# Expert tiles of a mixture of experts recorded by readiness of the engines, with lists of free PSUM halves, in place of a lockstep rotation

## The chip, the cores and the metric

The kernel runs on one core of a Trainium2 chip. The metric is the device time of one execution in microseconds; several executions are made and their median is given.

## The reference, cut to what matters

Two transformer layers work on x of 16 sequences, 512 tokens and 128 channels, all in fp32. The last part of the second layer is a mixture of eight experts, of which each token takes the one with the largest gate value:

```python
idx = jnp.argmax(logits, axis=-1)
for e in range(E):                      # E = 8, D = 128, DF = 512
    m = (idx == e)[:, None].astype(xf.dtype)
    h = jax.nn.relu(xf @ W1[e] + b1[e])
    out = out + m * (h @ W2[e] + b2[e])
...
z = _layer_norm(y + _moe(y, ...), g2, be2)
...
x = x + gb * z
```

y is a layer norm too (with weights g1 and be1), and gb and the residual x differ from sequence to sequence. The change touches only how these last lines are carried out.

## The kernel before, in words

The program has three parts. The first (to about 780 us) does the first layer and the attention of the second for 16 sequences, four of them in flight. The second (to about 1065 us) does the attention inside the expert block and routes: for each token it finds the expert and writes the token's number into a list in DRAM (`order`), in the region of that expert. It leaves in DRAM a table `token_rows` with three rows of 128 values for each token: the normalized y (R_X), the gate row (R_G) and the residual row (R_RES).

The third part works the experts off. Each expert's list is cut into tiles of TS = 256 tokens. The number of tokens of an expert is known only on the device, so 8192 / 256 + 7 = 39 tiles are planned (NSLOT), and a few small operations (L1157 to L1222) find for each tile its expert and its tokens. `take` and `put` then hold the token numbers of each tile, as offsets for gathering and scattering.

`expert_tile(s)` (L1226) is a generator: a chain of 15 steps with a `yield` between them. For tile s:

- two indirect DMAs issued on GpSimd (POOL) gather the rows of 2 x 128 tokens into `x_in` (L1229);
- ScalarE (ACT) reads the number of the expert into a register (L1236) and copies that expert's weights, 1029 columns, from `ex` into `w` (L1238);
- TensorE (PE) turns the two halves of y into `x_ps`, a half of the PSUM tile `turn_ps` (L1242); ACT scales and shifts them into `y` (L1245);
- PE makes the hidden layer, four products of 128 x 256, into `h_ps` (L1249); VectorE (DVE) takes the maximum with minus the bias into `hid` (L1259), which is the ReLU without the bias;
- PE makes the output product, four accumulating products, into `o_ps`, a half of `out_ps` (L1263); DVE adds the bias and y into `acc` (L1272);
- PE turns `acc` back into `a_ps`, another half of `turn_ps` (L1276); `stats` (L1012) makes the layer norm's figures on DVE (L1017, L1019, L1024, L1280) and ACT (the square root, L1022);
- ACT normalizes into `z` (L1284), DVE multiplies by the gate row and adds the residual (L1292, L1293);
- two indirect DMAs issued on POOL scatter the rows into the output (L1296).

The halves of `turn_ps` and `out_ps` go by the parity of s (`s % 2`). `h_ps` is a tile of a pool with two buffers. `x_in` has six buffers, `w`, `y` and `z` four, the others three.

What sets the order is `staggered(chains, 3)` (L151): in lockstep it advances every running chain by one step, and every third step it starts a new one. The tile framework takes the instructions in the order in which they are recorded, finds the waits between them from the tiles that they read and write, and places them on the engines; it can move an instruction ahead of others on its engine.

The first two parts are recorded by another helper, `queued(chains, apart, width)` (L118). It keeps up to `width` chains, each with a due time, and advances the one that is due first. A chain yields what its step costs: "V1.2" is 1.2 us of DVE (V), P is PE, A is ACT, G is GpSimd, D a delay on no engine; parts with | run beside each other, parts with ; after each other, and a part with + isn't waited for. The helper books these costs on each engine and so sets the chain's next due time. `taken(free)` (L217) is a step that a chain repeats, at a cost of "D0.5", until a list has a free entry, which it then takes.

Of the kernel before, what the change touches and what calls it, by code (L numbers as in the profile page):

```python
# [21 lines left out]
F32 = mybir.dt.float32  # L22
# [6 lines left out]
P = 128  # L29
B, T, C = 16, 512, 128  # L30
# [3 lines left out]
NFC = DF // P  # L34
# [14 lines left out]
DEN_EPS = 1e-6  # L49
NEG = -1e30  # L50
TS = 2 * P
NSLOT = B * T // TS + NE - 1
REGION = B * T
R_X, R_G, R_RES, R_END = np.cumsum([0, C, C, C]).tolist()
E_W1, E_W2, E_NB1, E_OUT, E_END = np.cumsum([0, DF, DF, NFC, 1]).tolist()
# [62 lines left out]
def queued(chains, apart, width):  # L118

    chains, running, begin, free = iter(chains), [], 0.0, 0.0
    until = dict.fromkeys("PVAG", 0.0)
    while True:
        while len(running) < width and (chain := next(chains, None)) is not None:
            running.append([max(begin, free), chain])
            begin = running[-1][0] + apart
        if not running:  # L130
            return
        first = min(running, key=lambda entry: entry[0])
        took = next(first[1], None)
        if took is None:
            assert first is running[0], "a chain's buffers are those of the one that ends first"
            running.remove(first)
            free = first[0]
            continue
        for stage in took.split(";"):
            ends = [first[0]]  # L140
            for part in stage.split("|"):
                engine, us = part.lstrip("+")[0], float(part.lstrip("+")[1:])
                end = max(first[0], until.get(engine, 0.0)) + us
                if engine in until:
                    until[engine] = end
                if part[0] != "+":
                    ends.append(end)
            first[0] = max(ends) + 0.1


def staggered(chains, apart):  # L151

    chains, running, step = iter(chains), [], 0
    while True:
        if step % apart == 0 and (chain := next(chains, None)) is not None:
            running.append(chain)
        if not running:
            return
        for chain in list(running):
            if next(chain, chain) is chain:  # L160
                running.remove(chain)
        step += 1


@with_exitstack
def tile_adaln(ctx: ExitStack, tc: tile.TileContext, x, wa, wb, vec, wex, const, out):
# [50 lines left out]
    def taken(free):  # L217
        while not free:
            yield "D0.5"
        return free.pop(0)  # L220
# [790 lines left out]

    def stats(pool, src, n, tag):  # L1012

        st = pool.tile([P, n, 6], F32, tag=tag + "_st", name="st", bufs=3)
        mv = pool.tile([P, n, 2], F32, tag=tag + "_mv", name="mv", bufs=3)
        for g in range(n):
            nc.vector.bn_stats(st[:, g, :], src[:, g * C : (g + 1) * C])  # L1017
        for g in range(n):
            nc.vector.bn_aggr(mv[:, g, :], st[:, g, :])  # L1019
        yield  # L1020
        rs = pool.tile([P, n], F32, tag=tag + "_rs", name="rs", bufs=3)
        nc.scalar.activation(rs, mv[:, :, 1], AF.Sqrt, bias=lneps)  # L1022
        yield
        nc.vector.reciprocal(rs, rs)  # L1024
        return mv, rs

# [196 lines left out]

    out_rows = out.rearrange("b t c -> (b t) c")

    def expert_tile(s):  # L1226
        x_in = tp.tile([P, 2, R_END], F32, tag="x_in", name="x_in", bufs=6)
        for a in range(2):
            nc.gpsimd.indirect_dma_start(  # L1229
                out=x_in[:, a],  # L1230
                out_offset=None,
                in_=token_rows,
                in_offset=bass.IndirectOffsetOnAxis(ap=take[:, a, s : s + 1], axis=0),
            )
        yield
        e = nc.scalar.value_load(expert_i[0:1, s : s + 1], min_val=0, max_val=NE - 1)  # L1236
        w = tp.tile([P, E_END], F32, tag="w", name="w", bufs=4)
        nc.scalar.copy(w, ex[:, bass.ds(e, 1), :].rearrange("p a k -> p (a k)"))  # L1238
        yield
        x_ps = turn_ps[:, 0, s % 2]  # L1240
        for a in range(2):
            nc.tensor.transpose(x_ps[:, a * P : (a + 1) * P], x_in[:, a, R_X:R_G], ident)  # L1242
        yield
        y = tp.tile([P, TS], F32, tag="y", name="y", bufs=4)
        nc.scalar.activation(y, x_ps, AF.Identity, bias=v(V_BE1), scale=v(V_G1))  # L1245
        yield
        h_ps = sp.tile([P, NFC, TS], F32, tag="h_ps", name="h_ps")
        for f in range(NFC):
            mm(  # L1249
                h_ps[:, f, :],  # L1250
                lhsT=w[:, E_W1 + f * P : E_W1 + (f + 1) * P],
                rhs=y,
                start=True,
                stop=True,
            )
        yield

        hid = tp.tile([P, NFC, TS], F32, tag="hid", name="hid", bufs=3)
        tt(hid, h_ps, w[:, E_NB1:E_OUT].unsqueeze(2).to_broadcast([P, NFC, TS]), ALU.max)  # L1259
        yield  # L1260
        o_ps = out_ps[:, s % 2]
        for f in range(NFC):
            mm(  # L1263
                o_ps,
                lhsT=w[:, E_W2 + f * C : E_W2 + (f + 1) * C],
                rhs=hid[:, f, :],
                start=f == 0,
                stop=f == NFC - 1,
            )
        yield  # L1270
        acc = tp.tile([P, TS], F32, tag="acc", name="acc", bufs=3)
        stt(acc, o_ps, w[:, E_OUT:E_END], y, ALU.add, ALU.add)  # L1272
        yield
        a_ps = turn_ps[:, 1, s % 2]
        for a in range(2):
            nc.tensor.transpose(a_ps[:, a * P : (a + 1) * P], acc[:, a * P : (a + 1) * P], ident)  # L1276
        yield
        mv, rs = yield from stats(tp, a_ps, 2, "last")
        off = tp.tile([P, 2], F32, tag="off", name="off", bufs=3)
        stt(off, mv[:, :, 0], -1.0, rs, ALU.mult, ALU.mult)  # L1280
        yield
        z = tp.tile([P, 2, C], F32, tag="z", name="z", bufs=4)
        for a in range(2):
            nc.scalar.activation(  # L1284
                z[:, a],
                a_ps[:, a * P : (a + 1) * P],
                AF.Identity,
                bias=off[:, a : a + 1],
                scale=rs[:, a : a + 1],
            )  # L1290
        yield
        tt(z, z, x_in[:, :, R_G:R_RES], ALU.mult)  # L1292
        tt(z, z, x_in[:, :, R_RES:R_END], ALU.add)  # L1293
        yield
        for a in range(2):
            sent = nc.gpsimd.indirect_dma_start(  # L1296
                out=out_rows,
                out_offset=bass.IndirectOffsetOnAxis(ap=put[:, a, s : s + 1], axis=0),
                in_=z[:, a],
                in_offset=None,  # L1300
                bounds_check=B * T - 1,
                oob_is_err=False,
            )
            apart("out", sent.ins)

    staggered((expert_tile(s) for s in range(NSLOT)), 3)


# [90 lines left out]
```

## Time and profile before

| What | us |
|---|---|
| median of three runs | 1390.64 (1388.35 to 1391.99) |
| the profiled execution, its own time | 1304.73 |
| its span, first to last instruction | 1302.9 |
| first gather of an expert tile | 1080.64 |
| first scatter | 1105.76 |
| last gather | 1277.83 |
| last scatter | 1299.09 |

The profiled execution is 85.9 us shorter than the median of the runs. In the stretch of 178 us from 1106 to 1284, in which the tiles follow each other evenly, PE is busy 147.4 us, POOL 136.9, DVE 118.3 and ACT 92.3, at a granted TensorE clock of 1.00.

How to read the profile: a row of the timeline or of the groups names the engine, the line of the kernel, the operation, the tile written and the tiles read, the number of instructions, and in brackets the idle time of the engine just before and what ended it ("<-DVE hid L1259"). "issue" is time in which the engine waited for nothing that the profile shows. The 0.30 us between two indirect DMAs on POOL are of that kind. PEld is the loading of weights into TensorE, which lies beside PE's products. A product in fp32 appears as two records, so that four products make eight.

### The profile page before, as it was taken

The numbers are of one execution on the slowest core, as the hardware profiler recorded it, in microseconds if no ns is written. First come the engines' busy times: TensorE is split into PE (matmuls) and PEld (weight loads), VectorE is DVE, ScalarE is ACT, GpSimd is POOL, SyncE is SP. The second block draws the span as 40 slices with busy tenths as digits, with TensorE's granted clock in tenths as the row PEclk, the third lists the DMA queues.
The fourth block names the chain that finished last, engine by engine and source line by source line (L and its number), as shares of the span: only waits on it lengthen the run. The fifth ranks groups of instructions, "written<-read, shape, count | busy, mean of one in ns | idle before, by whom it ended". The sixth has DMA issues, their size and how long they took to land.

```text
span 1302.9 us, 37480 instructions
## 1 busy us (share of the span) xinstructions
PE 1022.4 (78%) x15605; PEld 742.7 (57%) x15605; DVE 814.8 (63%) x2335; ACT 645.7 (50%) x1116; POOL 576.5 (44%) x632
## 2 busy tenths in 40 slices
PE   3789899787798798898898786867687815888885
PEld 2467666565566566565765564655465514666663
DVE  7455877656666758667557765256667723666664
ACT  0535566455463555464365443255666613555552
POOL 5222434425323426324324343225555644777775
PEclk9877898888998889898689978587878757999998
DMA  4412323322332422333223224204423112333331
GB/s 156 114 33 52 86 52 88 73 60 58 86 57 64 95 49 71 81 65 85 58 56 74 48 52 159 66 26 36 41 40 49 24 19 77 97 98 97 101 98 39
DMA packets 155275, 90.62 MB, mean 70 GB/s; under 512 B 77070, under 2 KB 142609, under 8 KB 154976
## 3 DMA queue, kind: packets, MB, share of 16 engines
q1 hardware_dynamic: 144960, 65.36, 23.2%
q0 software_dynamic: 9568, 19.62, 5.5%
q8 instruction: 123, 2.02, 0.7%
q10 hardware_dynamic: 576, 3.23, 0.6%
q14 instruction: 48, 0.39, 0.1%
HBM read 47.96 MB, written 31.68 MB: 61 GB/s over the span
## 4 chain that ended last, share of the span: by engine, by line
PE 40%; DVE 27%; POOL 12%; ACT 7%; DMA 6%; issue 6%; SPq 0%; POOLq 0%; ACTq 0%; DVEq 0%
PE bank L464 5%; PE out_ps L1263 5%; PE h_ps L1249 4%; PE bank L533 4%; DVE q L406 3%; PE bank L630 3%; DVE hid L1259 3%; DVE sc L555 3%; POOL rs L403 2%; POOL order L1131 2%; PE scores L551 2%; DVE st L397 2%; DVE inc L595 2%; PE bank L617 2%; PE bank L420 2%
## 5 line engine op out<-in xcount | busy, mean ns | idle before, releaser
L533 PE MATMUL bank<-kh,q 32*32 32x128 f32 x4096 | 107.5, 315 | 14.4 <-DVE h L520 5.9
L406 DVE TENSOR_SCALAR q<-x,mv,rs 128x128 f32<-128x128 f32 x256 | 86.8, 396 | 42.2 <-POOL rs L403 42.1
L501 ACT ACTIVATE kh<-k,con 128x512 f32<-128x512 f32 x128 | 84.4, 715 | 50.3 <-POOL k L755 43.1
L533 PEld LDWEIGHTS bank<-kh,q 32*32 32x32 f32 x4096 | 81.9, 119 | 35.7 <-issue 9.5
L1263 PE MATMUL out_ps<-hid,w 128*128 128x256 f32 x312 | 77.6, 391 | 28.6 <-DVE hid L1259 28.3
L555 DVE TENSOR_TENSOR sc<-scores,con 128x1024 f32<-128x1024 f32 x64 | 77.4, 1210 | 35.5 <-PE scores L551 35.2
L607 POOL COPY states<-inc 32x576 f32<-32x576 f32 x64 | 43.7, 682 | 121.3 <-DVE inc L595 119.2
L1296 POOL DMA_INDIRECT out_x<-z,put x78 | 79.2, 1015 | 39.5 <-ACT rs L1022 17.9
L551 PE MATMUL scores<-ident,sc 128*128 128x128 f32 x512 | 80.7, 304 | 17.3 <-DVE sc L555 14.9
L542 ACT COPY sc<-bank 128x512 f32<-128x512 f32 x128 | 68.6, 588 | 46.9 <-PE bank L533 46.6
L1229 POOL DMA_INDIRECT x_in<-token_rows,take x78 | 77.3, 991 | 26.3 <-issue 18.9
L1131 POOL DMA_INDIRECT order<-con,idx x64 | 62.9, 983 | 50.6 <-DVE idx L1128 18.6
L551 PEld LDWEIGHTS scores<-ident,sc 128*128 128x128 f32 x512 | 66.0, 158 | 31.2 <-DVE sc L555 16.9
L1259 DVE TENSOR_TENSOR hid<-h_ps,w 128x1024 f32<-128x1024 f32 x39 | 47.8, 1225 | 54.4 <-PE h_ps L1249 54.4
L1263 PEld LDWEIGHTS out_ps<-hid,w 128*128 128x128 f32 x312 | 56.2, 190 | 43.1 <-DVE hid L1259 37.1
L630 PE MATMUL bank<-states,q 128*32 128x144 f32 x960 | 75.6, 425 | 6.0 <-POOL states L607 5.4
L422 ACT ACTIVATE h<-bank,mod 128x512 f32<-128x512 f32 x48 | 37.2, 775 | 83.1 <-PE bank L420 82.8
L1249 PE MATMUL h_ps<-y,w 128*128 128x256 f32 x312 | 76.2, 388 | 1.3 <-ACT y L1245 1.2
L1238 ACT COPY w<-ex 128x1029 f32 x39 | 40.8, 1052 | 67.2 <-DVE acc L1272 36.6
L617 PE MATMUL bank<-v_heads,sc 128*32 128x36 f32 x4096 | 62.3, 207 | 14.5 <-DVE sc L555 7.6
L607 ACT COPY states<-inc 32x576 f32<-32x576 f32 x64 | 42.8, 669 | 61.7 <-DVE inc L595 61.1
L617 PEld LDWEIGHTS bank<-v_heads,sc 128*32 128x32 f32 x4096 | 50.8, 115 | 37.8 <-issue 17.9
(248 smaller groups left out, 2539.6 us busy)
## 6 DMA issues: line engine op xcount, KB each, us to landing
v_rows<-values SPq DMA_DIRECT2D x32, 288.0 KB
v_chunks<-values SPq DMA_DIRECT2D x128, 72.0 KB
v_heads<-v_rows SPq DMA_DIRECT2D x128, 72.0 KB
gated<-mod_rows SPq DMA_DIRECT2D x16, 448.0 KB
x<-in_x SPq DMA_DIRECT2D x16, 256.0 KB
token_rows<-gated SPq DMA_DIRECT2D x16, 256.0 KB
token_rows<-ex SPq DMA_DIRECT2D x16, 256.0 KB
h_rows<-q SPq DMA_DIRECT2D x16, 256.0 KB
```

Of the source, the lines that this page charges most:

```text
L406: ts(xn[:, g, :], X[b][:, g, :], mv[:, g, 0:1], rs[:, g : g + 1], ALU.subtract, ALU.mult,)
L501: nc.scalar.activation(t[:, :, n, :], k.rearrange("p (n s) -> p n s", s=CH), AF.Copy, scale=con[:, K_HEAD + n : K_HEAD + n + 1],)
L533: mm(groups(s_ps[r])[c * CH : (c + 1) * CH, n], lhsT=by_block[rows, at], rhs=kh[rows, at].rearrange("p m s -> p (m s)"), start=True, stop= ...
L551: nc.tensor.transpose(groups(st_ps[:, r])[:, n], groups(sc[:, 2 * rr + r])[:, n], ident)
L555: tt(sc[:, 2 * rr : 2 * rr + 2].rearrange("p r (n t) -> p (r n) t", t=CH), st_ps.rearrange("p r (n t) -> p (r n) t", t=CH), causal.unsquee ...
L607: copy(state[rows, r], inc[rows])
L617: mm(o_ps[a][c * CH : (c + 1) * CH, k0 : k0 + RH * HV], lhsT=groups(sc[:, r])[:, g, c * CH : (c + 1) * CH], rhs=vh[:, g * NC + c, :, r * H ...
L630: mm(o_ps[a][c * CH : (c + 1) * CH, n * NH * HV : (n + 1) * NH * HV], lhsT=q.rearrange("p (n s) -> p n s", s=CH)[:, at_chunk(ch)], rhs=sta ...
L1131: put = nc.gpsimd.indirect_dma_start(out=order, out_offset=bass.IndirectOffsetOnAxis(ap=idx[:, g : g + 1], axis=0), in_=con[:, K_TOK + 4 * ...
L1249: mm(h_ps[:, f, :], lhsT=w[:, E_W1 + f * P : E_W1 + (f + 1) * P], rhs=y, start=True, stop=True,)
L1259: tt(hid, h_ps, w[:, E_NB1:E_OUT].unsqueeze(2).to_broadcast([P, NFC, TS]), ALU.max)
L1263: mm(o_ps, lhsT=w[:, E_W2 + f * C : E_W2 + (f + 1) * C], rhs=hid[:, f, :], start=f == 0, stop=f == NFC - 1,)
```

## The change

`staggered` is deleted, and the expert tiles are recorded by `queued`, with six chains in flight and 4.0 us between the starts of two. Every step yields its cost. The halves of PSUM are no longer chosen by parity: four lists hold the two free halves each of the turned input, the hidden product, the output product and the turned output. A chain takes a half ahead of the product that writes it and gives it back behind the last instruction that reads it. `h_ps` becomes two tiles of one buffer each; `turn_ps` and `out_ps` stay one tile each. The buffers of `x_in` and `z` go to eight, those of `w`, `y`, `hid`, `acc`, `off` and of the tiles of `stats` to seven. In `stats` two yields get costs. The computation is the same.

```diff
+SLOTS = 6
...
-def staggered(chains, apart):
...
-        st = pool.tile([P, n, 6], F32, tag=tag + "_st", name="st", bufs=3)
-        mv = pool.tile([P, n, 2], F32, tag=tag + "_mv", name="mv", bufs=3)
+        st = pool.tile([P, n, 6], F32, tag=tag + "_st", name="st", bufs=SLOTS + 1)
+        mv = pool.tile([P, n, 2], F32, tag=tag + "_mv", name="mv", bufs=SLOTS + 1)
...
-        yield
+        yield "V1.0"
...
+    free_in, free_hid, free_out, free_back = [0, 1], [0, 1], [0, 1], [0, 1]
+    h_banks = [sp.tile([P, NFC, TS], F32, tag=f"h_ps{n}", name="h_ps", bufs=1) for n in range(2)]
+
     def expert_tile(s):
-        x_in = tp.tile([P, 2, R_END], F32, tag="x_in", name="x_in", bufs=6)
+        x_in = tp.tile([P, 2, R_END], F32, tag="x_in", name="x_in", bufs=SLOTS + 2)
...
-        yield
+        yield "G2.2;D3.0"
         e = nc.scalar.value_load(expert_i[0:1, s : s + 1], min_val=0, max_val=NE - 1)
-        w = tp.tile([P, E_END], F32, tag="w", name="w", bufs=4)
+        w = tp.tile([P, E_END], F32, tag="w", name="w", bufs=SLOTS + 1)
         nc.scalar.copy(w, ex[:, bass.ds(e, 1), :].rearrange("p a k -> p (a k)"))
-        yield
-        x_ps = turn_ps[:, 0, s % 2]
+        yield "A1.2"
+        at = yield from taken(free_in)
+        x_ps = turn_ps[:, 0, at]
...
-        yield
+        yield "P0.4"
-        y = tp.tile([P, TS], F32, tag="y", name="y", bufs=4)
+        y = tp.tile([P, TS], F32, tag="y", name="y", bufs=SLOTS + 1)
         nc.scalar.activation(y, x_ps, AF.Identity, bias=v(V_BE1), scale=v(V_G1))
-        yield
-        h_ps = sp.tile([P, NFC, TS], F32, tag="h_ps", name="h_ps")
+        free_in.append(at)
+        yield "A0.6"
+        at = yield from taken(free_hid)
+        h_ps = h_banks[at]
...
+        yield "P1.9"
...
         tt(hid, h_ps, w[:, E_NB1:E_OUT].unsqueeze(2).to_broadcast([P, NFC, TS]), ALU.max)
-        yield
-        o_ps = out_ps[:, s % 2]
+        free_hid.append(at)
+        yield "V1.3"
+        at = yield from taken(free_out)
+        o_ps = out_ps[:, at]
...
+        yield "P2.0"
...
         stt(acc, o_ps, w[:, E_OUT:E_END], y, ALU.add, ALU.add)
-        yield
-        a_ps = turn_ps[:, 1, s % 2]
+        free_out.append(at)
+        yield "V0.5"
+        at = yield from taken(free_back)
+        a_ps = turn_ps[:, 1, at]
...
-        yield
+        free_back.append(at)
+        yield "A0.9"
         tt(z, z, x_in[:, :, R_G:R_RES], ALU.mult)
         tt(z, z, x_in[:, :, R_RES:R_END], ALU.add)
-        yield
+        yield "V0.7"
...
+        yield "G2.2"
...
-    staggered((expert_tile(s) for s in range(NSLOT)), 3)
+    queued((expert_tile(s) for s in range(NSLOT)), 4.0, SLOTS)
```

More of the change, by code (lines that the diff above doesn't have):

```diff
@@ L148, in queued @@
             first[0] = max(ends) + 0.1
-def staggered(chains, apart):
[L153 to L162, printed above, removed]
 @with_exitstack
@@ L1019, in stats @@
             nc.vector.bn_aggr(mv[:, g, :], st[:, g, :])
-        yield
-        rs = pool.tile([P, n], F32, tag=tag + "_rs", name="rs", bufs=3)
+        yield "V1.0"
+        rs = pool.tile([P, n], F32, tag=tag + "_rs", name="rs", bufs=SLOTS + 1)
         nc.scalar.activation(rs, mv[:, :, 1], AF.Sqrt, bias=lneps)
-        yield
+        yield "A0.3"
         nc.vector.reciprocal(rs, rs)
@@ L1255, in expert_tile @@
             )
-        yield
-        hid = tp.tile([P, NFC, TS], F32, tag="hid", name="hid", bufs=3)
+        yield "P1.9"
+        hid = tp.tile([P, NFC, TS], F32, tag="hid", name="hid", bufs=SLOTS + 1)
         tt(hid, h_ps, w[:, E_NB1:E_OUT].unsqueeze(2).to_broadcast([P, NFC, TS]), ALU.max)
-        yield
-        o_ps = out_ps[:, s % 2]
+        free_hid.append(at)
+        yield "V1.3"
+        at = yield from taken(free_out)
+        o_ps = out_ps[:, at]
         for f in range(NFC):
@@ L1269, in expert_tile @@
             )
-        yield
-        acc = tp.tile([P, TS], F32, tag="acc", name="acc", bufs=3)
+        yield "P2.0"
+        acc = tp.tile([P, TS], F32, tag="acc", name="acc", bufs=SLOTS + 1)
         stt(acc, o_ps, w[:, E_OUT:E_END], y, ALU.add, ALU.add)
-        yield
-        a_ps = turn_ps[:, 1, s % 2]
+        free_out.append(at)
+        yield "V0.5"
+        at = yield from taken(free_back)
+        a_ps = turn_ps[:, 1, at]
         for a in range(2):
             nc.tensor.transpose(a_ps[:, a * P : (a + 1) * P], acc[:, a * P : (a + 1) * P], ident)
-        yield
+        yield "P0.4"
         mv, rs = yield from stats(tp, a_ps, 2, "last")
-        off = tp.tile([P, 2], F32, tag="off", name="off", bufs=3)
+        off = tp.tile([P, 2], F32, tag="off", name="off", bufs=SLOTS + 1)
         stt(off, mv[:, :, 0], -1.0, rs, ALU.mult, ALU.mult)
-        yield
-        z = tp.tile([P, 2, C], F32, tag="z", name="z", bufs=4)
+        yield "V0.4"
+        z = tp.tile([P, 2, C], F32, tag="z", name="z", bufs=SLOTS + 2)
         for a in range(2):
@@ L1290, in expert_tile @@
             )
-        yield
+        free_back.append(at)
+        yield "A0.9"
         tt(z, z, x_in[:, :, R_G:R_RES], ALU.mult)
         tt(z, z, x_in[:, :, R_RES:R_END], ALU.add)
-        yield
+        yield "V0.7"
         for a in range(2):
```

## The prediction

> **What bounds the kernel now.** I read the busy time by stretches first. The expert tiles run from the first gather at 1080.64 us to the end at 1302.9, about 222 us. In their steady part no engine is full: per 10 us PE is busy 8.24, POOL 7.78, DVE 6.79, ACT 5.36, and the TensorE clock is granted at 1.00 (columns: stretch, length, PE, PEld, DVE, ACT, POOL, clock, DMA share, GB/s).
>
> ```profile
> 1185.00:1195.00 10.00, 8.24 (x42) 6.84 (x41) 6.79 (x21) 5.36 (x11) 7.78 (x8) 1.00 0.34 96
> ...
> 1275.00:1285.00 10.00, 8.66 (x39) 6.36 (x38) 6.31 (x20) 3.33 (x8) 7.07 (x7) 1.00 0.37 93
> ```
>
> So I looked at two loops. The chain of waits in order of time shows a ring of PE and DVE (start, us, what).
>
> ```profile
> 1184.17 1.99 PE out_ps L1263 x8
> 1186.16 1.74 PE h_ps L1249 x8
> 1187.93 1.24 DVE hid L1259
> 1189.21 1.99 PE out_ps L1263 x8
> ```
>
> One turn, 1184.17 to 1189.21, takes 5.04 us: the lockstep order puts the hidden product of one tile behind the output product of the one before and makes both wait for the ReLU. The timeline of POOL shows the second loop.
>
> ```profile
> 1094.47 0.95 POOL L1229 DMA_INDIRECT x_in<-token_rows,take  x1 [0.30 <-issue]
> 1105.76 1.03 POOL L1296 DMA_INDIRECT out_x<-z,put  x1 [10.34 <-ACT rs L1022]
> 1107.09 1.00 POOL L1296 DMA_INDIRECT out_x<-z,put  x1 [0.31 <-issue]
> 1108.40 1.00 POOL L1229 DMA_INDIRECT x_in<-token_rows,take  x1 [0.30 <-issue]
> ...
> 1279.11 1.14 POOL L1296 DMA_INDIRECT out_x<-z,put  x1 [0.30 <-ACT y L1245]
> 1280.56 1.00 POOL L1296 DMA_INDIRECT out_x<-z,put  x1 [0.30 <-issue]
> ...
> 1285.33 0.98 POOL L1296 DMA_INDIRECT out_x<-z,put  x1 [1.20 <-ACT rs L1022]
> ...
> 1289.64 0.98 POOL L1296 DMA_INDIRECT out_x<-z,put  x1 [2.05 <-ACT rs L1022]
> ...
> 1299.09 0.98 POOL L1296 DMA_INDIRECT out_x<-z,put  x1 [1.81 <-issue]
> ```
>
> Each tile needs two gathers and two scatters, each about 1.0 us of POOL with 0.30 between. From tile 0's first scatter (1105.76) to tile 33's (1279.11) lie 33 tiles or 132 issues in 173.35 us: 1.313 us an issue, 5.25 a tile, and no gap there is above 0.31. POOL, at 5.25, is slower than the ring of 5.04. That it shows 78% is only because the 0.30 is not counted. It stands still only at the ends: 10.34 us after 12 gathers, and 1.20, 2.05 and 1.84 among the last scatters.
>
> [...] all 156 are on POOL, so they can't be shared out by a new order. [...] the trace shows the price, 1.31 us an issue. [...]
>
> **The change part by part.** Everything ahead of the first gather is the same program, instruction by instruction and wait by wait, so 1080.64 us stand. Nothing is removed or added within the tiles either: 156 indirect DMAs, the same products, the same copies. What changes is order and buffers.
>
> (1) Gathers ahead. With eight x_in buffers in place of six the built POOL order holds 16 gathers ahead of the first scatter, not 12, and 16 scatters at its end, not 12. Gathers alone are 1.257 us apart (1080.64 to 1094.47 in 11 steps), so 16 end near 1080.64 + 16 x 1.257 = 1100.8, inside the old stand of 10.34 us. Four issues so leave the saturated part: 4 x 1.313 = 5.25 us.
>
> (2) The first scatter. Tile 0's chain (gather, turn, hidden and output product, statistics, z) is as long as before. On DVE the built order has the two products by the gate (L1292, L1293 of before) directly behind the third ReLU, ahead of the next tile's two BN_STATS (0.50 us together). I take 0.5 us: scatter at 1105.3.
>
> (3) The rest is counted at POOL's pace: 140 issues are left, 139 steps from the first to the last: 1105.3 + 139 x 1.313 = 1287.8. The unexplained 1.81 ahead of the very last issue is 1.5 over the usual 0.30; I leave it in: 1289.3. Before it was 1299.09. Without any new stall this is 9.8 us less; about 4 of it are the stands of the tail, which go since 16 scatters (21 us) now lie behind the last gather, and cover most of the last tile's chain (about 4.1 us from issue to landing in the chain of waits, then 13.2 us, 1281.95 to 1295.14).
>
> (4) What the new order makes late. The rotation by parity becomes lists of free halves, but turn_ps and out_ps stay one tile each, and the waits in the built program are on the whole tile: a bias add (L1272) whose tile has its half complete still waits for the output product written into the other half, if that is ahead of it in the recorded order. In 10 places two bias adds now follow each other on DVE, the first waiting for the second's product. One such wait is one more output product, 1.99 us. Queued behind it on DVE are that tile's statistics, and on ACT its z; who waits is POOL with the scatter. The first comes at tiles 2 and 3, when POOL has no work in hand: I charge 2.0 in full. At tiles 8 and 9 the scatters stand as four in a row ahead of four gathers, so tile 8's may be late again: between 0 and 2, taken 1.0. From then on I charge nothing for the other pairs: the products alone start 1.83 + 1.73 + 0.18 + 0.18 = 3.9 us a tile (distances between starts of L1263, L1249, L1276, L1242), 1.3 below POOL, and with eight gathers ahead a tile has 42 us (8 x 5.25) for its chain. If that cover is gone each costs up to 2 us. Tail: the last chain just fits; 0 to 2.6, taken 1.2.
>
> (5) More w, y, hid, acc, st, z buffers: ACT's wait of the w copy for acc (36.6 us in the waits) goes, worth 0, since POOL, not ACT, bounds. ACT loses no time for the register loads that the built order draws forward: in before two of them and more lie inside waits.
>
> Sum: -9.8 + 2.0 + 1.0 + 1.2 = -5.6 us. Of the profiled execution (1304.73, span 1302.9 and 1.8 around it) this makes 1299.1. The median of the runs, 1390.64, is 85.9 above that execution, and no view says where. I carry the difference over unscaled: 1385.0. (Scaled by 1.066 it would be 5.9.)
>
> **The rivals.** B, much faster: the runs are 6.6% longer than the profiled execution; if that is a slower TensorE, the ring and not POOL bounds them. At 0.8 of the clock a turn is (1.99 + 1.74) / 0.8 + 1.31 = 5.97 us, 0.72 over POOL, and setting it free is worth up to 34 x 0.72 = 24 us more: 1361. For it: PE makes up 40% of the chain over the program, and the granted clock has a mean of 0.861. Against it: in this stage the clock is 1.00, a uniform slowdown moves POOL as well, and the pairs of (4) grow with the products.
>
> C, slower: late outputs. POOL is always behind, so time it loses to a late z never comes back. If all ten pairs hit it for 2.0 us, that is 20 against the 9.8: +10.2, 1401. It decides from 9.8 us of stands, and is slower beyond measurement from 14. For it: in before z was ready every 5.04 us, evenly, which no list of readiness keeps. Against it: the slack of 1.3 us a tile outside the first few tiles.
>
> D, nothing: stands of 6 to 14 us eat the gain; 1389 or so. The estimates of durations that drive the new order (2.2 us for two gathers) are below the 2.6 of the trace, so POOL is believed ahead of where it is.
>
> **How the numbers follow.** About 0.3%, 4.2 us, is what a measurement of this kernel can tell from no change. The forecast A, 1382 to 1388, has 0.58, of which a fifth lies under 4.2 us; B 0.12; D 0.18; C 0.12. Faster: 0.46 + 0.12, say 0.57; same 0.12 + 0.18, say 0.31; slower 0.12. The range reaches from the middle of B to the edge of C: 1367 to 1394.
>
> **What would show it.** Right: 16 gathers spaced 1.26, first scatter near 1105, then 1.31 a step with one stand of about 2 us near the third tile's scatter, last scatter near 1293 to 1294; the ring of L1263, L1249 and L1259 no longer unbroken in the chain, POOL in its place. Wrong: stands of POOL all along (C, D), or a steady pace below 5.25 a tile, which would mean that the 1.31 is not POOL's own. Wrong too if the first scatter comes later than 1106 because ACT copies w for eight tiles ahead of tile 0's z.

## The result, and the profile after

The changed kernel is slower, by less than 2%. On the runs beside which the prediction was made it takes 1410.4 us in the median (1408.2 to 1411.8) against 1389.5 of the kernel before: a ratio of 1.016, 95% interval 1.012 to 1.020. Measured twice more it took 1396.2 against 1383.3 (1.008, 1.005 to 1.011) and 1395.6 against 1380.6 (1.009, 1.006 to 1.012). The prediction had 1385.0. The ratios here and below are estimated from the executions outside a slower state and need not be the quotients of the medians.

One thing has to be known for all numbers below: the executions fell on three chips, on which the same program does not take the same time. On the first chip (e0 to e3 and all runs named f and g) the kernel before takes 1381 to 1392 us in the median, and on the third (h1 and h2) 1392.0. On the second (e4 to e7) it takes 1304.7 us (63 runs, 1290 to 1316). For the first timed runs and for the profile that the prediction read the chip is not on record: by their times the runs (1389.5 and 1410.4) are of the first chip's kind and the profile (1304.73) is of the second's.

The profiled execution of the changed kernel takes 1410.47 us, its span 1408.7. Its timeline of POOL (start, us busy, what, and in brackets the idle time just before) answers to the one shown of before:

```profile
1139.06 0.95 POOL L1220 DMA_INDIRECT x_in<-token_rows,take  x1 [0.30 <-issue]
1140.31 0.95 POOL L1220 DMA_INDIRECT x_in<-token_rows,take  x1 [0.30 <-issue]
1154.97 1.03 POOL L1295 DMA_INDIRECT out_x<-z,put  x1 [13.71 <-issue]
1156.31 1.01 POOL L1295 DMA_INDIRECT out_x<-z,put  x1 [0.31 <-issue]
1157.62 1.00 POOL L1220 DMA_INDIRECT x_in<-token_rows,take  x1 [0.30 <-issue]
...
1171.75 1.01 POOL L1295 DMA_INDIRECT out_x<-z,put  x1 [6.61 <-issue]
...
1370.40 1.01 POOL L1295 DMA_INDIRECT out_x<-z,put  x1 [6.85 <-ACT rs L1009]
...
1404.91 0.98 POOL L1295 DMA_INDIRECT out_x<-z,put  x1 [0.85 <-issue]
```

The 16 gathers ahead are there, 1.26 us apart as predicted. But the first scatter comes 33.5 us after the first gather (1121.46), not 24.7, and then POOL does not keep going: it stands for 13.7, 6.6, 6.9 us and more. One issue still costs 1.31 us where it follows another. In the groups of the page the idle time ahead of the scatters is 105.6 us:

```profile
L1295 POOL DMA_INDIRECT out_x<-z,put x78 | 78.3, 1004 | 105.6 <-issue 45.7
```

The busy times by stretches (columns as before: stretch, length, PE, PEld, DVE, ACT, POOL, clock, DMA share, GB/s) show two kinds of stretch instead of one:

```profile
1185.00:1195.00 10.00, 7.83 (x37) 6.03 (x36) 4.68 (x16) 4.17 (x9) 7.82 (x8) 1.00 0.34 94
1225.00:1235.00 10.00, 3.03 (x16) 2.10 (x14) 3.54 (x16) 3.74 (x7) 7.68 (x8) 0.91 0.43 118
1275.00:1285.00 10.00, 6.33 (x19) 5.05 (x20) 3.52 (x13) 4.21 (x8) 2.98 (x3) 0.53 0.18 57
```

In the second line PE, DVE and ACT are each busy for a third of the time while POOL issues its eight; in the third the TensorE clock is 0.53, and PE's 19 records fill 6.3 us. What happens there is seen in the timeline around 1230 us:

```profile
1228.14 1.89 PE L1243 MATMUL h_ps<-y,w 128*128 128x256 f32 x8
...
1229.87 0.38 PE L1234 MATMUL turn_ps<-ident,x_in 128*128 128x128 f32 x2
...
1230.30 1.00 POOL L1295 DMA_INDIRECT out_x<-z,put  x1 [0.30 <-ACT rs L1009]
1231.60 1.00 POOL L1220 DMA_INDIRECT x_in<-token_rows,take  x1 [0.30 <-DMA out_x<-z,put]
1232.90 0.98 POOL L1220 DMA_INDIRECT x_in<-token_rows,take  x1 [0.30 <-issue]
1234.19 1.01 POOL L1295 DMA_INDIRECT out_x<-z,put  x1 [0.30 <-issue]
1234.92 1.22 DVE L1253 TENSOR_TENSOR hid<-h_ps,w 128x1024 f32<-128x1024 f32 x1 [4.68 <-remote]
...
1237.05 0.56 ACT L1237 ACTIVATE y<-turn_ps,vec_sb 128x256 f32<-128x256 f32 x1 [7.01 <-remote]
...
1237.66 1.65 PE L1243 MATMUL h_ps<-y,w 128*128 128x256 f32 x3 [7.41 <-ACT y L1237]
```

The hidden product ends at 1230.03 by the trace, and DVE is free, but the ReLU that waits for it starts at 1234.92. The turn of x_in ends at 1230.25, and y, which waits for it, starts at 1237.05. In the trace "remote" means that the wait ended with a semaphore's update just before the start, but that no instruction's end fits that update. I call such a wait late: a DVE or ACT instruction among the expert tiles starts more than 0.5 us after both its own engine is free and the last product that the built program makes it wait for has ended. This execution has 24 of them, 66 us together, and in the first profile of before there is not one. PE stands through them, and its clock falls: the granted clock is 1.00 from 1137 to 1140 us and 0.50 from 1143 to 1149, and the eight records (four products) of L1259 that took 1.99 us at 1134.64 take 3.78 at 1145.26, after 5.66 us of idle PE. A caution: the ends of the products in this profile are modelled. So one such wait alone can't tell whether the product is late or only the news of it.

### The profile page after: what moved, and what is told of

The parts are those of the page before. It is cut to its first block, busy times and chain, and to the rows that moved or that the text cites. A ratio compares the mean times of both kernels' runs of the same rounds, so it can differ in the third digit from the quotient of the medians.

```text
span 1408.7 us, 37474 instructions
## 1 busy us (share of the span) xinstructions
PE 1052.5 (75%) x15605; PEld 755.5 (54%) x15605; DVE 812.4 (58%) x2335; ACT 639.2 (45%) x1116; POOL 576.3 (41%) x632
## 5 line engine op out<-in xcount | busy, mean ns | idle before, releaser
L1295 POOL DMA_INDIRECT out_x<-z,put x78 | 78.3, 1004 | 105.6 <-issue 45.7
L520 PE MATMUL bank<-kh,q 32*32 32x128 f32 x4096 | 103.7, 308 | 14.9 <-DVE h L507 6.0
L1259 PE MATMUL out_ps<-hid,w 128*128 128x256 f32 x312 | 88.2, 426 | 31.9 <-DVE hid L1253 25.0
L1243 PE MATMUL h_ps<-y,w 128*128 128x256 f32 x312 | 90.9, 441 | 22.1 <-ACT y L1237 14.1
L520 PEld LDWEIGHTS bank<-kh,q 32*32 32x32 f32 x4096 | 78.7, 116 | 34.9 <-issue 9.7
L1259 PEld LDWEIGHTS out_ps<-hid,w 128*128 128x128 f32 x312 | 63.4, 213 | 46.9 <-DVE hid L1253 29.1
L1220 POOL DMA_INDIRECT x_in<-token_rows,take x78 | 77.0, 987 | 26.5 <-issue 22.3
L1243 PEld LDWEIGHTS h_ps<-y,w 128*128 128x128 f32 x312 | 67.4, 225 | 37.6 <-ACT y L1237 16.5
```

Source lines behind the costliest of these rows:

```text
L520: mm(groups(s_ps[r])[c * CH : (c + 1) * CH, n], lhsT=by_block[rows, at], rhs=kh[rows, at].rearrange("p m s -> p (m s)"), start=True, stop= ...
L1220: nc.gpsimd.indirect_dma_start(out=x_in[:, a], out_offset=None, in_=token_rows, in_offset=bass.IndirectOffsetOnAxis(ap=take[:, a, s : s + ...
L1243: mm(h_ps[:, f, :], lhsT=w[:, E_W1 + f * P : E_W1 + (f + 1) * P], rhs=y, start=True, stop=True,)
L1259: mm(o_ps, lhsT=w[:, E_W2 + f * C : E_W2 + (f + 1) * C], rhs=hid[:, f, :], start=f == 0, stop=f == NFC - 1,)
L1295: sent = nc.gpsimd.indirect_dma_start(out=out_rows, out_offset=bass.IndirectOffsetOnAxis(ap=put[:, a, s : s + 1], axis=0), in_=z[:, a], in ...
```

## The experiments

The first question was whether the change makes the lateness, or whether it was there before.

**Four runs on the first chip.** The kernel before again; before with the buffers alone (`bufs` of x_in and z 8, of w, y, hid, acc, off, st, mv and rs 7); the changed kernel with PSUM tiles of their own:

```diff
-    turn_ps = sp.tile([P, 2, 2, TS], F32, tag="turn", name="turn_ps", bufs=1)
-    out_ps = sp.tile([P, 2, TS], F32, tag="out", name="out_ps", bufs=1)
+    turn_in = sp.tile([P, 2, TS], F32, tag="turn_in", name="turn_in", bufs=1)
+    turn_back = sp.tile([P, 2, TS], F32, tag="turn_back", name="turn_back", bufs=1)
+    out_banks = [
+        sp.tile([P, 2, TS], F32, tag=f"out{n}", name=f"out_ps{n}", bufs=1) for n in range(2)
+    ]
...
-        o_ps = out_ps[:, at]
+        o_ps = out_banks[at][:, 0]
```

and the changed kernel with a regular order:

```diff
-    queued((expert_tile(s) for s in range(NSLOT)), 4.0, SLOTS)
+    queued((expert_tile(s) for s in range(NSLOT)), 5.3, SLOTS)
```

> The kernel before, unchanged, profiled once more, because the execution that was profiled first (1304.7 us) lies 85 us under the median of the timed ones (1389.5). Theory O (order): the new order of issue makes POOL stand, and the lockstep order does not; so wherever the 85 us of a usual execution lie, the expert tiles of the lockstep kernel take about 222 us from first gather to last scatter again, with about 40 us of idle time ahead of the scatters, and the rest is found in the stages ahead of the first gather. Theory E (execution): a usual execution of any of the two kernels has stretches in which results of TensorE come late, in the expert tiles too; then the profile of the kernel before shows 1385 to 1392 us, the expert tiles in 255 us or more, and 80 us or more of idle time ahead of the scatters.

> The lockstep order with the larger buffers of the changed kernel (x_in and z 8, w, y, hid, acc and the statistics 7). The prediction charged the buffers nothing: within 0.3% of the kernel before, 1385 to 1394 us. If buffers held something back in a usual execution, 1375 or less. Theory O and theory E both expect no change from the kernel before, since the order of issue stays.

> The changed kernel with four PSUM tiles in place of two: the turns of x and those of acc each have a bank as a tile of their own, and each half of the out products has a bank of its own, so that the waits of one tile's bias add or normalisation on another tile's products (whole-tile waits) are gone, while the order of issue stays. If the whole-tile waits are what the changed order made costly (step 4 of the prediction, rival C): ten pairs at 2 us and more, so 1380 to 1392 us. If the order itself, or late results of TensorE, cost the time: 1405 to 1412 us.

> The changed kernel with the chains begun 5.3 instead of 4.0 units apart. The built order then repeats tile for tile on TensorE, VectorE and POOL through the middle (each out product in one piece, one bias add at a time, 3 instructions of gathers and 6 of scatters in turn), still with 16 gathers ahead of the first scatter and six tiles in flight. If the irregular order makes POOL stand (theory O): 1383 to 1392 us, the idle time ahead of the scatters down from 105.6 us to 60 or less. If an execution's late results set the time whatever the order (theory E): 1403 to 1412 us with 90 us or more of it.

| run | median us | ratio to before, 95% interval | late waits, us | idle ahead of scatters |
|---|---|---|---|---|
| e0_before | 1391.8 | 1.000 (0.998 to 1.003) | 31, 73 | 89.2 |
| e1_buffers | 1394.7 | 1.003 (0.999 to 1.006) | 28, 76 | 102.8 |
| e2_own_banks | 1399.4 | 1.011 (1.004 to 1.018) | 37, 110 | 103.7 |
| e3_apart53 | 1391.4 | 1.001 (0.996 to 1.005) | 18, 52 | 99.9 |

Theory E holds for the kernel before: on this chip it too has late waits all along, the expert tiles take 267.6 us from first gather to last scatter instead of 218.5, and POOL stands ahead of the scatters for 89.2 us instead of 39.5. Its timeline:

```profile
1270.83 1.89 PE L1249 MATMUL h_ps<-y,w 128*128 128x256 f32 x8
...
1273.50 0.38 PE L1242 MATMUL turn_ps<-ident,x_in 128*128 128x128 f32 x2
1274.33 1.00 POOL L1229 DMA_INDIRECT x_in<-token_rows,take  x1 [0.30 <-issue]
1275.63 0.98 POOL L1229 DMA_INDIRECT x_in<-token_rows,take  x1 [0.30 <-issue]
1277.71 1.23 DVE L1259 TENSOR_TENSOR hid<-h_ps,w 128x1024 f32<-128x1024 f32 x1 [4.54 <-remote]
1278.49 0.81 ACT L1284 ACTIVATE z<-turn_ps,off,rs 128x128 f32<-128x128 f32 x2 [4.24 <-remote]
1278.99 0.80 PE L1263 MATMUL out_ps<-hid,w 128*128 128x256 f32 x1 [5.11 <-DVE hid L1259]
```

The stretches of the two profiles of before say where the chips part. First the one that the prediction read, then e0_before; the third part of each begins near the first indirect DMA of the routing (876.9 and 882.8 us), the fifth is the expert tiles:

```profile
0.00:780.00 780.00, 651.60 (x12658) 457.85 (x12659) 510.03 (x1352) 394.94 (x657) 284.95 (x326) 0.88 0.31 71
...
876.00:1067.00 191.00, 133.49 (x1282) 96.19 (x1282) 122.50 (x462) 107.96 (x202) 108.33 (x120) 0.76 0.29 36
...
1105.00:1302.00 197.00, 153.37 (x723) 124.31 (x721) 125.92 (x373) 95.89 (x181) 145.05 (x144) 0.98 0.31 88
```

```profile
0.00:780.00 780.00, 650.38 (x12606) 456.23 (x12606) 505.14 (x1347) 392.47 (x653) 284.05 (x324) 0.87 0.30 71
...
876.00:1104.00 228.00, 147.64 (x1307) 101.08 (x1305) 127.38 (x474) 111.87 (x208) 109.26 (x121) 0.74 0.21 32
...
1145.00:1390.00 245.00, 167.73 (x722) 133.81 (x720) 125.91 (x372) 95.79 (x181) 144.52 (x144) 0.91 0.25 71
```

Up to the first indirect DMA the two are alike but for 6 us. From there to the first gather of a tile, which is the routing, lie 203.7 and 237.0 us, and from the first gather to the last scatter 218.5 and 267.6: together 82 of the 88 us, and these are the parts in which GpSimd issues indirect DMAs. In the routing of e0_before too seven waits of DVE and ACT end in "remote" (28 us), and none in the first profile. The program up to the first gather is nearly the same in all runs, and the chips part in it as well: the routing took 226 to 245 us in the profiles on the first chip and 197 to 207 on the second, where e5, e6 and e7 have one or two such waits in it, of 3.4 us at most.

Theory O falls in what it said of the lockstep kernel, and is right on the order: with chains 5.3 apart the loss is not seen here (a later run has 0.4% of it), though the idle time ahead of the scatters stays at 99.9 us where 60 were expected. The buffers alone cost nothing that can be told from zero. Banks of their own alone end between the two expectations, at 1.1%; the interval, 1394.5 to 1415.1 us on the 1389.5 of before, reaches into that of the order or of late results and not into that of the whole-tile waits, which are so not shown to be the cause. And no kernel gains, though e1 and e3 have the 16 gathers ahead.

**Plain transfers, and both edits together.** In three of the next four the indirect DMAs of the expert tiles were replaced, so that these leave out the choice of the rows:

```diff
-            nc.gpsimd.indirect_dma_start(
-                out=x_in[:, a],
...
+            row0 = (2 * s + a) * P % (B * T)
+            nc.sync.dma_start(out=x_in[:, a], in_=token_rows[row0 : row0 + P, :])
...
-            sent = nc.gpsimd.indirect_dma_start(
-                out=out_rows,
...
+            row0 = (2 * s + a) * P
+            to = out_rows if s < B * T // TS else spare
+            row0 %= B * T
+            sent = nc.sync.dma_start(out=to[row0 : row0 + P, :], in_=z[:, a])
```

e4 has the first half, e5 both on the kernel before, e6 both on the changed one; e7 is the changed kernel with banks of its own and 5.3.

> The kernel before (lockstep) with the gathers of x_in replaced by plain transfers of 128 consecutive rows on SyncE's queue: it leaves out the choice of the rows, so its output is of other tokens; the scatters stay. In usual executions of both kernels VectorE and ScalarE wait for products that the trace shows as ended 2 to 5 us earlier, and such waits occur only from the first indirect transfer on. Theory L (late signals come with GpSimd's indirect transfers): half of these are gone, so at most half of the 73 us of late waits stay, GpSimd (1.31 us an issue, 2.6 a tile) bounds nothing, and the time is 1340 to 1365 us. Theory K (the products themselves are slow, because of TensorE's clock or its order): late waits stay as they are, 1380 to 1392 us.

> The kernel before (lockstep) with the gathers of x_in and the scatters of z both replaced by plain transfers of 128 consecutive rows on SyncE's queue (tiles 32 to 38 to a spare buffer): it leaves out the choice of the rows on both sides, and no indirect transfer is left among the expert tiles. Theory L: no late wait is left there, TensorE's clock stays at 1.0, and 39 tiles take the ring of 5.04 us each: some 197 us and 15 of filling, 210 in place of 268, so 1328 to 1342 us. Theory K: late waits stay, 1375 us or more.

> The changed kernel with the same replacement on both sides (the choice of the rows left out, no indirect transfer among the expert tiles). It tells whether the new order of issue costs time by itself or only where it meets late results. Order alone (theory O, and rival C of the prediction: out products wait for bias adds two at a time): slower than the lockstep kernel with the same replacement by 15 us or more. Order only as the carrier of lateness: within 5 us of it, 1328 to 1345 us.

> The changed kernel with both edits that were tried one at a time: the four PSUM tiles with banks of their own, and the chains 5.3 units apart. One of them alone gave 1391.4 us (order regular), the other 1399.4 us (banks). If whole-tile waits still cost time under the regular order: 1378 to 1388 us, a faster kernel than both. If the regular order leaves nothing for them to cost: 1388 to 1395 us, the same as the kernel before.

They ran on the second chip, where the kernel before took 1304.7 us: e4 1302.9 (ratio 0.999, 0.997 to 1.002), e5 1298.4 (0.997, 0.994 to 1.001), e6 1297.9 (0.994, 0.992 to 0.997), e7 1291.1 (0.992, 0.989 to 0.995). None has a late wait, so theories L and K can't be told apart there, and the times expected, which were for the first chip, don't apply. What follows all the same: without lateness the new order by itself costs nothing that the medians show (e6 against e5; their profiles have 222.4 and 219.2 us from the first load of x_in to the last store, so 3 us more), and the changed kernel with both edits is 0.8% faster there. POOL's timeline of e7:

```profile
1097.77 1.17 POOL L1223 DMA_INDIRECT x_in<-token_rows,take  x1 [0.30 <-issue]
1099.24 1.03 POOL L1298 DMA_INDIRECT out_x<-z,put  x1 [0.30 <-issue]
...
1283.61 0.98 POOL L1298 DMA_INDIRECT out_x<-z,put  x1 [2.20 <-issue]
```

The first scatter follows the 16th gather without a stand, and the last comes 184.4 us later: 139 steps of 1.313 make 182.5, and the one stand left is 1.9 over the usual 0.30.

**The same on the first chip.** f1 is the changed kernel again; f2, f3 and f4 are e5, e6 and e7.

> The changed kernel itself once more. The runs so far fell on two chips: on the first the kernel before takes 1389.5 us (and 1391.8 in its own profile), on the second 1304.7 us, which is what its first profile showed; on the second no wait for a product ends late. On a chip like the second, the prediction's sum was made for this case: theory P (the sum holds where no result comes late): 1304.7 - 5.6 = 1299 us, 1290 to 1302. Theory O (the order itself makes GpSimd stand): 1315 us or more there too. On a chip like the first: 1406 to 1412 us again.

> The lockstep kernel with plain transfers in place of gathers and scatters (the choice of the rows left out on both sides). On a chip where results come late (kernel before at 1389.5): theory L (late signals come with GpSimd's indirect transfers): none is late among the expert tiles, 210 in place of 268 us there, 1328 to 1342 us. Theory K (products slow in themselves on that chip): late waits stay, 1375 us or more. On a chip like the second: 1298 us again.

> The changed kernel with plain transfers on both sides (the choice of the rows left out). On a chip where results come late: if the order costs time only as the carrier of lateness, within 5 us of the lockstep kernel with the same transfers; if the order costs by itself there, slower than it by 15 us or more. On a chip like the second: 1298 us again.

> The changed kernel with PSUM banks of its own for each use and chains 5.3 units apart. On a chip where results come late: the regular order with 16 gathers ahead gave no gain there (1391.4 us), so 1383 to 1393 us; if the whole-tile waits add to the lateness, 1382 us or less. On a chip like the second: 1291 us again.

This time it was the first chip (before 1383.3). f2 took 1324.5 us (0.958, 0.951 to 0.965), a little under the 1328 to 1342 expected, with no late wait, at a TensorE clock of 1.00 from 1140 to 1260 us: theory L, and K falls. Its routing keeps its indirect DMAs, and there 13 waits still end in "remote" (44 us) and the 227.7 us stand against 197.3 in e5: that is what is left of the difference between the chips, 26 us where the kernel before has 79. f3 took 1330.5 (0.962, 0.955 to 0.969), also without a late wait. It is 6 us above f2; the intervals of the ratios overlap, but each of its four runs (1327.7 to 1335.1) lies above each of f2's (1321.0 to 1327.4), so a part of the loss may be the order's own. f1 was slower again, though by less than the 1406 to 1412 us expected (1396.2, 1.008; 25 late waits, 67 us), f4 at 1388.6 within 0.5% (1.003, 1.001 to 1.006; 27 late waits, 62 us): on this chip the two edits bring the changed kernel back, and no further. The waits of DVE, from e0_before and then f2 (columns: us in total, times, longest):

```profile
DVE hid L1259 <- remote: 23.6, 7, 4.5
...
DVE acc L1272 <- remote: 7.7, 6, 3.1
```

```profile
DVE hid L1256 <- PE h_ps L1246: 53.5, 39, 7.2
```

In f2 all 39 tiles have the same wait for their own hidden product, and no line ends in "remote".

**Which transfers.** g1 is the changed kernel and g2 is e3 again; g3 is e4 (plain gathers), g4 has plain scatters alone.

> The changed kernel once more, for a chip on which no product is signalled late (kernel before at about 1304.7 us): theory P (the prediction's sum holds there): 1290 to 1302 us. Theory O (the order makes GpSimd stand by itself): 1315 us or more. On a chip with late results: 0.8 to 1.6% slower than the kernel before, as twice measured.

> The changed kernel with chains 5.3 units apart (regular order, whole-tile waits kept). On a chip without late results the run with banks of its own on top of it gave 1291.1 us against 1304.7: if the banks play no part, 1289 to 1294 us; if they do, between that and g1. On a chip with late results: within 0.5% of the kernel before, as once measured.

> The lockstep kernel with plain transfers in place of the gathers alone (the choice of the rows of x_in left out). On a chip with late results, where 267.6 us among the expert tiles fell to about 210 with plain transfers on both sides: if every indirect transfer brings its share, about half of the 59 us goes: 1345 to 1365 us; if lateness needs a GpSimd that issues without a break, all of it: 1330 us or less; if the scatters alone bring it, 1375 us or more. On the other chip: 1303 us again.

> The lockstep kernel with plain transfers in place of the scatters alone (the choice of the output's rows left out; tiles 32 to 38 go to a spare buffer). On a chip with late results: if every indirect transfer brings its share, 1345 to 1365 us; if it needs a GpSimd that issues without a break, 1330 us or less; if the gathers alone bring it, 1375 us or more. On the other chip: 1298 to 1304 us.

It was the first chip again (before 1380.6). g1: 1395.6 (1.009). g2: 1389.3 (1.004, 1.000 to 1.008; 18 late waits, 48 us), 6 us under g1. g3: 1331.9 (0.963, 0.961 to 0.965), no late wait. g4: 1326.9 (0.960, 0.957 to 0.963), two, 3 us. Taking away either half takes away nearly all the lateness: on this chip it does not come issue by issue, but with four indirect issues a tile (31 late waits, 73 us, in e0_before; 5.25 us of POOL a tile at the 1.313 us of the first profile).

**Other work between the issues.** The last two runs move the end of each tile to GpSimd, where it stands between two gathers and two scatters; h2 moves L1292 as well.

```diff
-        tt(z, z, x_in[:, :, R_RES:R_END], ALU.add)
+        nc.gpsimd.tensor_tensor(z, z, x_in[:, :, R_RES:R_END], ALU.add)
```

> The lockstep kernel with the last addition of each tile (L1293, 0.43 us on VectorE) moved to GpSimd, where it stands between two gathers and two scatters: about 0.65 us by GpSimd's rows of 128x512 (1.04 to 1.37 us, halved), so 5.9 us of GpSimd's work a tile in place of 5.25. Theory B (late signals need indirect issues back to back, and get through when GpSimd does something else): late waits for products fall from about 31 to 15 or fewer, 39 tiles at 5.9 us and 25 of filling are 255 in place of 268 us, so 8 to 15 us faster than the kernel before on the first chip. Theory M (the load of indirect transfers matters, not what stands between): late waits stay, and the addition costs 0 to 25 us. On a chip without late results: 15 to 25 us slower.

> The lockstep kernel with both last operations of each tile (L1292 and L1293) on GpSimd between two gathers and two scatters: some 1.3 us, 6.55 us a tile. Theory B: few late waits left (5 or fewer), 39 x 6.55 + 25 = 280 us among the expert tiles, 5 to 15 us slower than the kernel before. Theory M: late waits stay, and 20 us slower or more. On a chip without late results: 40 to 55 us slower.

On the third chip (before 1392.0) h1 took 1363.0 us (0.981, 0.970 to 0.992) with 9 late waits of 11 us together, h2 1389.4 (1.000, 0.998 to 1.003) with one of 3 us. Theory B has the fewer late waits in both and the sign of h1, which gained more than the 8 to 15 us expected; h2 cost nothing where 5 to 15 us were expected. Two things limit this. The kernel before was not profiled on this chip, so the 31 late waits that these are held against are the first chip's. And the edit does three things at once: it puts other work between the issues, it spaces them out (5.91 us a tile instead of 5.25), and it takes 0.42 us a tile from DVE. A GpSimd that only pauses was not run, so which of the three counts is not shown. In the groups of POOL in h1 the scatters and the addition read (busy us, mean ns of one, then the idle time just before and what ended it):

```profile
L1296 POOL DMA_INDIRECT out_x<-z,put x78 | 78.0, 999 | 26.5 <-issue 23.4 <-POOL z L1293 2.8 <-DVE mv L1019 0.3
...
L1293 POOL TENSOR_TENSOR z<-z,x_in 128x256 f32<-128x256 f32 x39 | 29.0, 743 | 11.2 <-DVE mv L1019 9.8 <-issue 0.8
```

Here the 26.5 us are little more than the 78 gaps of 0.30, and the stand for the first scatter and for z has gone to the addition's row. POOL now sets the pace, 5.91 us a tile, and that is a steadier pace than 5.25 with stands. In h2 it is 6.75, and the 33 us that this adds over 39 tiles eat the gain. h1 has the lowest ratio to the kernel before, on a chip of the slower kind, of the kernels that leave nothing out; the changed kernel was not run beside it. Nor was h1 run on the second chip, where up to the 29.0 us of its own row would come on top of POOL's work (an estimate).

## Why the prediction was wrong, by its own steps

**The premise, and the step that failed.** "POOL is always behind" was read rightly from the profile: 132 issues in 173.35 us with no gap. But that was one execution of 1304.73 us, of the second chip's kind, and the last step, "I carry the difference over unscaled", took its bound along with its time to runs of 1390 us. The text noted that no view said where the 85.9 us lay, and gave a chance of 0.12 to one reading of them (rival B, a slower TensorE). In e0_before they lie in the routing and among the expert tiles, where the late waits are, and with these POOL is not the bound: it stands for 66 us above its own pace (89.2 ahead of the scatters, less 78 gaps of 0.30), against 16 in the first profile. No gain from fewer POOL issues is then seen (e1, e3).

**(1), gathers ahead, -5.25 us.** The 16 gathers came, the gain did not: e1 and e3 have them too, at 1.003 and 1.001. On the second chip e7, which has them with two more edits, bears the step out.

**(2), first scatter 0.5 us earlier.** It comes 33.5 us after the first gather instead of 24.7 (33.4 and 32.0 in f1 and g1; 25.6 in e0_before). It is 33.8 in e1, which has the 16 gathers and the lockstep order, and 30.2 and 30.4 in e3 and g2, so on this chip a late first scatter is seen with the 16 gathers in either order. A run of 16 gathers without a break is itself a run of indirect issues: two waits in it or just behind it are late, 1.8 us at 1138.40 and 5.1 us at 1143.98, and the eight records of 3.78 us, at a clock of 0.50, follow.

**(3), the rest at POOL's pace.** 139 steps of 1.313 make 182.5 us; the profiled execution took 249.9 from first to last scatter. This is the term that was off most. The forecast had that stretch 9.3 us shorter than before; against e0_before (242.0) it is 7.9 longer, and with the 7.9 us of (2) the tiles of this execution are 15.8 us longer than those of e0_before. These are single executions, though: from first gather to last scatter f1 and g1 have 281.7 and 274.7 us, and e1, whose median is not told apart from before, has 281.0 against the 267.6 of e0_before. A few us between two profiles therefore carry little here; the medians carry the verdicts. e7 took 184.4 on the second chip, so the pace was counted rightly for the chip that the profile showed, but for the timed runs it was not the pace.

**(4), what the new order makes late, +4.2 us.** "From then on I charge nothing" relied on 1.3 us a tile of spare time outside POOL. With late results that cover is gone, since POOL stands for its scatters, and the sentence after it, "if that cover is gone each costs up to 2 us", was the nearer case. Its size, though, is not that of whole-tile waits: e2 takes them away and is still at 1.011. That the larger part of the loss hangs on the order is shown by the distance of the starts, the only thing that differs in e3 (1.001) and g2 (1.004, 6 us under g1); f4, with banks of its own besides, is 8 us under f1. Whether the regular repetition helps or only the wider spacing is not told apart by one distance. How the order costs the time is not shown either. The number of late waits doesn't explain it, 24 and 25 in the changed kernel against 31. Who waits doesn't either: in the lockstep kernel 15 of the 31 are those of z (L1284), at the end of a tile, and none of y; in the changed kernel five are those of y (L1237), 18 us together, and y is what the next hidden product of PE needs. But the waits of y that end in "remote", five in the changed kernel (27.1 us of idle time), are four in e3 (15.9) and seven in f4 (22.8), and these two don't have the loss of about 1%. POOL's longest stands are 13.7, 11.1 and 9.5 us, against 10.9, 5.9 and 4.9 in e0_before and 10.5, 7.1 and 6.9 in e3; but g2 has 11.4, 10.6 and 7.1, so this doesn't settle it.

**(5), buffers: 0.** Right within its interval (1.003, 0.999 to 1.006).

**The rivals.** The sign and nearly the size are those of rival C (1401), and its sign in the profile, stands of POOL all along, came. Its mechanism did not: POOL is not always behind, and the pairs of bias adds are not what costs. Rival B looked for the missing 86 us in a slower TensorE; the clock among the expert tiles (1145 to 1385 us) is indeed 0.87 in the changed kernel and 0.92 in e0_before, but it goes with the late waits: without one it is 1.00 in f2 (1140 to 1260 us) and in the first profile of before (1105 to 1285 us); and setting the ring free gained nothing.

What stays open: the changed kernel itself was never run on the second chip, so whether its -5.6 us hold there is not known; e6 and e7 only say that the order costs little and that with two edits it gains. Nor is it known why a product is noticed late on one chip and not on another. That the signal is late, and not the product, is seen at one place in e1_buffers: a ReLU and a normalisation wait for products that ended at 1267.3 and 1269.9 by the trace, and start at 1272.93 and 1273.05. Behind the first product PE has four turns, which take it 0.66 us from the first start to the last end (1269.22 to 1269.88), and the last of which is the second product; were the first product itself late, and the four turns behind it as in the trace, the second wait could not end 0.12 us after the first. The trace's record of the semaphores agrees: the four updates for products that start between 1266.94 and 1269.60 stand within 0.11 us, 1272.91 to 1273.02. What holds them up is not known.

## What to carry to other kernels

Compare the profiled execution's own time with the timed median before you read a bound from it; if they differ as here (85.9 us, 6.6%), the bound belongs to that execution alone, and the first experiment is a second profile of the unchanged kernel. Where engines wait with no releaser in the trace while GpSimd issues indirect DMAs one behind the other, try other GpSimd work between the issues: 0.74 us a tile was worth 1.9% here (0.8 to 3.0; whether by the work or by the spacing that it brings is not shown). And an order written by estimated readiness should be tried at more than one distance of the starts; here the distance (5.3 instead of 4.0) decided between a loss of about 1% and one of 0 to 0.4%.

## What the runs showed of the hardware

Three chips ran the same program in 1304.7, in 1381 to 1392 and in 1392.0 us, with the first indirect DMA of the routing at 872 to 883 us on all of them. On the first chip, DVE and ACT started up to 4.5 us (kernel before) or 7.5 us (changed kernel) after the modelled end of the product they waited for, 31 times among 39 tiles in the kernel before, when GpSimd issued four indirect DMAs a tile (1.31 us each); with two a tile it was 0 or 2 times (g3, g4), with none 0 times (f2, f3). On the third chip, with 0.74 us of other work between the gathers and the scatters, it was 9 times (h1). On the second chip it was 0 times with four a tile (e7).
